# Wo's last weight sums, the first batch's inverse roots and the end's stores and routing in a fused post-LN layer

## The chip, the core and the metric

The kernel runs on one core of one Trainium2 chip, in one launch. The metric is device time in microseconds (us), as the median of three runs. The engines named below are PE (TensorE, matrix products), PEld (its weight loads), DVE (VectorE), ACT (ScalarE), POOL (GpSimd) and SP (SyncE, which issues most DMAs). All of them work through their own instructions in order; semaphores hold an instruction until its inputs are there and its output tile is free.

## The reference

Two batches of 512 tokens with 512 features pass through one layer, all in float32:

```python
q, k, v = (x @ W + b for Wq, Wk, Wv)          # 32 query heads, 8 key/value groups, 128 wide; rope on q and k
probs = softmax(causal(q k^T / sqrt(128)))
x1 = layernorm(x + (probs v) @ Wo + bo)
y  = x1 @ W_base^T + b_base
alpha = softmax(log(prior + eps) + x1 @ router_W^T + router_b)   # over 4 active experts
y += 2 * sum_e alpha_e * (x1 @ A_e^T) @ B_e^T                    # rank 8 each
out = layernorm(x1 + y)
```

A layernorm needs, per token, the mean, the variance and the inverse root of variance plus 1e-5.

## The kernel before

**Stages.** After a setup (about the first 60 us of the profile) comes a long loop over slots `T`. A slot scores 32 query rows of four heads against the keys (L546), and in the same slot come the row maxima (L554, DVE), exponentials (L561, ACT), normalisation (L569) and transposes (L577, L579) of slots just before, the weighing of values (L602), projections of later heads, and the output projection of earlier ones. Sixteen slots are one unit (one key group of one batch); there are 16 units, so 256 slots, `T_END = 256`. Four slots make one part, 128 tokens of four heads; a part's probabilities go out to DRAM and come back transposed (L587, L595, on SP). The order within a slot is written out by hand in `slot(T)`, and single steps are put at the end of a slot with `put(T, f)`; the schedule is taken as written. So every engine's order is the program's order.

**Products with seven instead of eight block multiplications.** Projections and the output projection use Strassen's scheme on 2 x 2 blocks, which needs sums of weight blocks and of data blocks first. For Wo these are `wo_sums`: four subtractions of 128x512 elements per set (L627), on DVE, into a tile `wt` of three blocks (`t1`, `t2`, `t4`; one buffer) and one in place (`b12`). A set is one key group's part of Wo. Sets 0 to 5 serve two units each; sets 6 to 9 serve one each. `wo_products` (L434) uses set `n` from slot `wo_from(first unit) = 16 u + 21`: its third product reads `t2` two slots on, the fourth reads `t1`, the fifth `b12`, the sixth `t4`. The sums of the data side, `ctx_sums` (L421 to L424), are on POOL, in the last slot before each new pair of heads. `rope_step` (L368, L371, L375 on DVE; L376 on POOL) and `w_sums` (L421 to L424 on POOL) run in the same slots. The last two units' output projection is plain (`wo_mm`, L674), so only sets 0 to 7 have sums, and only sets 6 and 7 of them serve a single unit (12 and 13).

**The second half of the layer.** The four token tiles of the first batch are finished while the second batch's last units are still in attention: `Ffn.stats` (L693, L694), `Norm.root` (an ACT square root at L697 and a DVE reciprocal at L698), `centre` (L701), `transpose` (L275, L276), `base` (L745), `logits`/`alphas` (L762 to L776), `low_rank`, `finish`, `add` (L796). They are put at slots counted from `A = 245`. Statistics of tiles 0 and 1 are at `A - 7` and `A - 6`, of 2 and 3 at `A`; one root for all four at `A + 1`. ACT holds the function tables of either the exponential or the square root, and an `ACT_TABLE_LOAD` stands before each change between them.

**The end.** After the loop the rest is written out line by line: `fz` is the first batch's last tile, `fa[0]`, `fa[1]`, `fb`, `fc` are the four tiles of the second batch in the order in which they end. `fc` is routed apart from its base product (`route`, L755: eight matmuls of 16 or 20 columns), and its base product is taken in two halves (L804) so that its statistics start early. Before the change the roots of `fz`, `fa[0]` and `fa[1]` stand together after `fa[1].add()`, followed by three stores (POOL applies the norm at L701, SP issues the DMA), and only then come `fb.logits()` and `fb.alphas()`.

Of the kernel before, what the change touches and what calls it, by code (L numbers as in the profile page):

```python
# [9 lines left out]
F32 = mybir.dt.float32  # L10
I32 = mybir.dt.int32
AF = mybir.ActivationFunctionType
ALU = mybir.AluOpType
AX = mybir.AxisListType

P = 128
# [7 lines left out]
LN_EPS = 1e-5  # L24
# [5 lines left out]
def postln_layer_kernel(  # L30
# [33 lines left out]
    nc = tc.nc  # L64
    B, S, HID = x.shape
    NT = B * S // P
    TPB = S // P
    KC = HID // P
    E_TOT, RK, _ = lora_A.shape
    O = W_base.shape[0]  # L70
    OC = O // P
    EA = active.shape[0]
    EAR = EA * RK
# [19 lines left out]
    def set_of(u):  # L93
        return u // B if u < MIXED else MIXED // B + u - MIXED

    def set_units(n):
        return [u for u in range(NU) if set_of(u) == n]
# [23 lines left out]
    OH, ARH = O // 2, EAR // 2  # L121
    WX_COLS = OH + ARH + EA
    arT = const.tile([P, KC, EAR + EA], F32, name="arT")
# [35 lines left out]
    def load_wo(n):  # L159
        wo_g = wow.tile([P, R, HID], F32, tag="wo_g", name=f"wo_{n}")  # L160
        nc.sync.dma_start(out=wo_g, in_=Wo[ts(sets[n], R * D), :].rearrange("(r p) n -> p r n", p=P))
        wos[n] = wo_g
# [455 lines left out]
    def wo_block(n, c_half, n_half):  # L618
        return wos[n][:, CH * c_half : CH * (c_half + 1), ts(n_half, NHALF)]

    def wo_sums(n, step):

        if step == 0:
            wt[n] = wow.tile([P, 3, CH, NHALF], F32, tag="wt", name=f"wt_{n}", bufs=1)
        t1, t2, t4 = (wt[n][:, m] for m in range(3))
        b11, b12, b21, b22 = (wo_block(n, c_half, n_half) for c_half in range(2) for n_half in range(2))
        nc.vector.tensor_tensor(  # L627
            *((t1, b12, b11), (t2, b22, t1), (b12, b22, b12), (t4, b21, t2))[step], ALU.subtract)

    def ctx_block(k, head, c_half):  # L630
# [52 lines left out]
    class Norm:  # L683
# [10 lines left out]
            nc.vector.bn_aggr(self.mv[:, i, :], st)  # L694

        def root(self, lo, hi):
            nc.scalar.activation(self.rstd[:, lo:hi], self.mv[:, lo:hi, 1], AF.Sqrt, bias=eps_sb)  # L697
            nc.vector.reciprocal(self.rstd[:, lo:hi], self.rstd[:, lo:hi])  # L698

        def apply(self, i, dst, src=None, engine=nc.vector):  # L700
            engine.tensor_scalar(  # L701
                dst, dst if src is None else src, self.mv[:, i, 0:1], self.rstd[:, i : i + 1], ALU.subtract, ALU.mult)
# [8 lines left out]
    class Ffn:  # L711
# [28 lines left out]
        def base(self, c):  # L740
            if c == 0:
                self.new_banks()
            for n in range(2):
                w = OH + (ARH, WX_COLS - OH)[n]
                nc.tensor.matmul(  # L745
                    self.py[n][:, :w], lhsT=self.xT[:, c, :], rhs=wbT[:, c, n, :w], start=(c == 0), stop=(c == KC - 1),
                    skip_group_check=True)

        def route(self, pool, tag):

            zl = pool.tile([P, 2, WX_COLS - OH], F32, tag=tag, name="zl")
            for n in range(2):
                w = (ARH, WX_COLS - OH)[n]
                for c in range(KC):
                    nc.tensor.matmul(  # L755
                        zl[:, n, :w], lhsT=self.xT[:, c, :], rhs=wbT[:, c, n, OH : OH + w],
                        start=(c == 0), stop=(c == KC - 1))
            self.z = [zl[:, n, :] for n in range(2)]

        def logits(self):  # L760
            self.lg = self.own([P, EA], "lg")
# [81 lines left out]
    def put(slot, f):  # L843
        extra.setdefault(slot, []).append(f)
# [59 lines left out]
    def wo_from(u):  # L904
        return UNIT * u + LAG_WO

    for n in range(2, NSETS):
        put(wo_from(set_units(n - 2)[-1] + 1) + 1, lambda n=n: load_wo(n))
    for n in range(NSETS - 2):
        for k in range(4):  # L910
            put(wo_from(set_units(n)[0]) + (0, 1, 1, 3)[k], lambda n=n, k=k: wo_sums(n, k))


    weigh_at = {}
# [139 lines left out]
    wbT = ffn_pool.tile([P, KC, 2, WX_COLS], F32, name="wbT")  # L1054
# [9 lines left out]
    def tiles(ts_, banks, name):  # L1064
        n = len(ts_)
        norms = Norm(ffn_pool, n, f"a{name}"), Norm(ffn_pool, n, f"f{name}")
        return [Ffn(t, bank, *norms, i) for i, (t, bank) in enumerate(zip(ts_, banks))]

    f0 = tiles(range(TPB), ((QX, QY), (QX, QY), (SC, SC), (QX, QY)), "0")
    fa = tiles([TPB + i for i in order[:2]], ((SC, SC), (WX, WY)), "1a")  # L1070
# [3 lines left out]
    A = LAST + LAG_WO  # L1074

    def transposed_base(c):
        transpose_token_tile(wbT[:, :, c // 2, ts(c % 2, P)], wb_sb[:, c, :], ps_k, "k", nc.scalar.copy)

    for c in range(OC):
        put(T_PROJ + (0, 1, 4, 5)[c], lambda c=c: nc.sync.dma_start(out=wb_sb[:, c, :], in_=W_base[ts(c, P), :]))  # L1080
        put(T_PROJ + (4, 5, 8, 9)[c], lambda c=c: transposed_base(c))
    put(A + 1, lambda: f0[0].norm1.root(0, TPB))
    for k, f in enumerate(f0):
        put(A + (-7, -6, 0, 0)[k], f.stats)
        put(A + 1 + k // 2, f.centre)
        put(A + 3 + k // 2, lambda f=f, k=k: f.transpose(*(QX, QY)[k % 2]))
    for f, at in zip(f0, (A + 5, A + 11, A + 13)):
# [11 lines left out]
    fz = f0[3]  # L1099
# [37 lines left out]
    fz.finish()  # L1137
    fc.transpose(*CTX)
    fz.add()
    base(fa[1])  # L1140
    fa[0].low_rank()
    fc.route(*CTX)
# [3 lines left out]
    fa[1].alphas()  # L1146
    fa[0].finish()
    fa[0].add()
    for c in range(KC):
        fb.base(c)  # L1150
        if c == 2:
            fa[1].low_rank()
    fc.low_rank()
    fa[1].finish()
    fa[1].add()
    fz.norm2.root(3, TPB)
    fa[0].norm2.root(0, 2)
    for f in (fz, *fa):
        f.store()
    fb.logits()  # L1160
    fb.alphas()
    for c in range(KC):
        fc.half(0, c)
    fc.half_end(0)
    fc.half_stats(0)
    fb.low_rank()
    for c in range(KC):
        fc.half(1, c)
# [59 lines left out]
```

## Time and profile before

| what | value |
|---|---|
| median of 3 runs | 831.65 us (830.76 to 831.83) |
| the profiled execution's own time | 829.5 us |
| its span, first to last recorded work | 827.4 us |
| PE, PEld busy | 99%, 72% |
| DVE, ACT, POOL busy | 73%, 46%, 38% |
| granted TensorE clock, mean | 0.998 |

The profile is of one execution. "Busy" is the time in which an engine has an instruction running; for PE the ends of matmuls are modelled, so the distance between starts is the better measure. Rows of the timeline give start, duration, engine, line and operation, output <- input, shape, count, and in brackets the idle time of the engine just before and what ended it. A float32 matmul is recorded as two rows, so "x4" of L434 is two matmuls.

### The profile page before, as it was taken

Reading aid. Unit: us, or ns where it says so; the run is one execution under the profiler, and the core shown is the slowest. Engines: PE = TensorE matmul, PEld = TensorE weight load, DVE = VectorE, ACT = ScalarE, POOL = GpSimd, SP = SyncE. Lnnn points to the kernel's source line nnn. Section 1 sums busy time; section 2 is a strip of 40 time slices with the busy share of each in tenths; the row PEclk is TensorE's granted clock in tenths of the full one; section 3 lists DMA queues with packets and bytes.
Section 4 is the critical chain, followed back from the end, with each engine's and each line's share of the span. In section 5 each row is a group of like instructions: output and inputs, shape, how many; then the busy total and the mean of one; then the engine's idle time right before and its main releaser. Section 6 shows DMA issues by size and latency. Waiting matters only on the chain.

```text
span 827.4 us, 11161 instructions
## 1 busy us (share of the span) xinstructions
PE 816.1 (99%) x3389; PEld 597.5 (72%) x3389; DVE 602.3 (73%) x1964; ACT 378.8 (46%) x1058; POOL 313.7 (38%) x342
## 2 busy tenths in 40 slices
PE   9999999999999999999999999999999999999996
PEld 5567777777777778787778778777778776645574
DVE  5368877677879886787768786787768789854545
ACT  1236454444545454444445354444445454663133
POOL 6464344421534345322533245442534433300032
PEclk9999999999999999999999999999999999999999
DMA  9015627444464547264554536374544546574211
GB/s 295 31 55 150 201 75 203 108 127 153 128 170 136 178 96 227 70 175 121 153 142 123 169 97 207 89 218 130 153 128 135 171 95 202 164 248 119 64 38 64
DMA packets 84413, 115.98 MB, mean 140 GB/s; under 512 B 6525, under 2 KB 64237, under 8 KB 82306
## 3 DMA queue, kind: packets, MB, share of 16 engines
q1 hardware_dynamic: 83682, 114.98, 48.2%
q8 instruction: 27, 0.44, 0.2%
q0 software_dynamic: 448, 0.14, 0.2%
q14 instruction: 32, 0.26, 0.1%
q10 hardware_dynamic: 224, 0.16, 0.1%
HBM read 71.21 MB, written 44.04 MB: 139 GB/s over the span
## 4 chain that ended last, share of the span: by engine, by line
PE 93%; DVE 4%; ACT 2%; issue 1%; POOL 1%; DVEq 0%; POOLq 0%
PE pc L602 16%; PE sc L546 14%; PE qx L434 11%; PE wx L434 11%; PE qy L434 9%; PE wy L434 8%; PE pp L355 5%; PE kx L434 4%; PE vx L512 4%; PE py L745 3%; PE po L674 3%; PE pv L338 3%; PE tp L275 1%; PE py L790 1%; DVE sc L554 0%
## 5 line engine op out<-in xcount | busy, mean ns | idle before, releaser
L554 DVE CUSTOM_DVE_ANT_0 sc<-sc,maskw 128x288 f32<-128x288 f32 (+15 forms) x256 | 114.2, 446 | 141.9 <-PE sc L546 140.3
L561 ACT ACTIVATE p<-sc,nmax 128x288 f32<-128x288 f32 (+15 forms) x256 | 124.1, 485 | 203.1 <-DVE nmax L554 180.9
L602 PE MATMUL pc<-pT,v 128*128 128x512 f32 x320 | 165.5, 599 | 0.0
L546 PE MATMUL sc<-kT,qT 128*128 128x160 f32 (+15 forms) x512 | 162.2, 399 | 1.7 <-ACT p L561 1.7
L376 POOL TENSOR_TENSOR qT<-q,t 128x512 f32<-128x512 f32 x56 | 76.9, 1372 | 179.9 <-DVE q L375 179.9
L569 ACT ACTIVATE p<-p,den 128x288 f32<-128x288 f32 (+15 forms) x256 | 133.2, 521 | 0.1
L546 PEld LDWEIGHTS sc<-kT,qT 128*128 128x128 f32 x512 | 95.9, 190 | 25.5 <-issue 8.6
L609 ACT ACTIVATE ctxT<-pc,bqkT 128x512 f32<-128x512 f32 x64 | 44.0, 687 | 116.4 <-PE pc L602 116.4
L421 POOL TENSOR_TENSOR cs<-ctxT 128x256 f32<-128x256 f32 x28 | 22.2, 794 | 157.8 <-PE wy L434 93.7
L577 DVE STREAM_TRANSPOSE zt<-p 128x128 f32<-128x128 f32 (+2 forms) x192 | 81.7, 425 | 0.0
L602 PEld LDWEIGHTS pc<-pT,v 128*128 128x128 f32 x320 | 57.0, 190 | 18.9 <-issue 5.7
L470 ACT COPY q<-qx 128x256 f32<-128x256 f32 x112 | 41.3, 369 | 36.6 <-PE qx L434 36.6
L434 PE MATMUL qx<-xs,wq 128*128 128x256 f32 x224 | 58.0, 381 | 0.0
L434 PE MATMUL wx<-wo,ctxT 128*128 128x256 f32 x224 | 57.6, 380 | 0.0
L434 PEld LDWEIGHTS qx<-xs,wq 128*128 128x128 f32 x224 | 41.4, 190 | 22.3 <-issue 18.4
L579 DVE STREAM_TRANSPOSE zt<-p 128x32 f32<-128x32 f32 (+3 forms) x256 | 57.5, 225 | 0.0
L561 ACT ACTIVATION_READ_ACCUMULATOR p<-sc,nmax 128x1 f32 x256 | 49.8, 195 | 0.0
L434 PEld LDWEIGHTS wx<-wo,ctxT 128*128 128x128 f32 x224 | 42.4, 190 | 7.8 <-issue 1.3
L660 DVE TENSOR_TENSOR x_sb<-wx,x_sb 128x256 f32<-128x256 f32 x112 | 47.0, 420 | 0.0
L368 DVE SCALAR_TENSOR_TENSOR t<-q,bqkT,rope_sb 64x512 f32<-64x512 f32 x56 | 45.0, 804 | 1.5
L701 POOL TENSOR_SCALAR y<-y,mv_f,rstd_f 128x512 f32<-128x512 f32 x4 | 8.5, 2129 | 94.2 <-DVE rstd_f L698 94.2
L371 DVE SCALAR_TENSOR_TENSOR t<-q,bqkT,rope_sb 64x512 f32<-64x512 f32 x56 | 42.2, 754 | 1.3
(215 smaller groups left out, 1505.7 us busy)
## 6 DMA issues: line engine op xcount, KB each, us to landing
db<-zt SPq DMA_DIRECT2D x64, 256.0 KB, 4.1
pT<-db SPq DMA_DIRECT2D x16, 1024.0 KB, 4.8
db<-zt SPq DMA_DIRECT2D x64, 192.0 KB, 3.1
pT<-db SPq DMA_DIRECT2D x16, 768.0 KB, 4.3
wq<-in_L_attn_Wq_dram SPq DMA_DIRECT2D x20, 512.0 KB, 5.3
wo<-in_L_attn_Wo_dram SPq DMA_DIRECT2D x10, 1024.0 KB, 7.6
db<-zt SPq DMA_DIRECT2D x64, 128.0 KB, 2.4
pT<-db SPq DMA_DIRECT2D x16, 512.0 KB, 4.0
```

The lines of the kernel that those rows point to most:

```text
L368: nc.vector.scalar_tensor_tensor(t2[lo, :], q[hi, :], b_ap[hi, :], rope_sb[hi, 1, :], ALU.add, ALU.mult)
L376: nc.gpsimd.tensor_tensor(dst, t1[:, :].rearrange("p (n s) -> p n s", s=BLK), t2[:, :].rearrange("p (n s) -> p n s", s=BLK), ALU.add)
L434: nc.tensor.matmul(ps, lhsT=wt[:, c, :], rhs=xt[:, c, :], start=start and c == 0, stop=c == CH - 1, skip_group_check=True)
L546: nc.tensor.matmul(sc[s][:, :w], lhsT=qT[u][:, i * QB + n].rearrange("p r s -> p (r s)"), rhs=kT[u][:].rearrange("p n s -> p (n s)")[:, :w ...
L554: nc.vector.tensor_tensor_reduce(sc[s][:, :w], sc[s][:, :w], maskw[:, S - w :], -SCALE, -MASKED, ALU.add, ALU.min, nmax[s])
L561: nc.scalar.activation(ptile[s][:, :w], sc[s][:, :w], AF.Exp, bias=nmax[s], scale=-1.0, accum_out=rden[s])
L569: nc.scalar.activation(ptile[s][:, :w], ptile[s][:, :w], AF.Copy, scale=rden[s])
L577: nc.vector.transpose(z[:, :, last - i : last, n, :].rearrange("p q j s -> p j q s"), ptile[s][:, : i * P])
L579: nc.vector.transpose(z[:, : n + 1, last, n, :], ptile[s][:, i * P : w])
L602: nc.tensor.matmul(psc[p], lhsT=v_sb[g // VG, b][:, j, ts(g % VG, D)], rhs=pT[p][:, :, ts(j, P)], start=(j == 0), stop=(j == i))
L609: nc.scalar.activation(ctxT[p], psc[p], AF.Identity, bias=bqkT[:, col : col + 1])
L660: nc.vector.tensor_tensor(into, pw[k, bank], into, ALU.add)
```

## The change

- `wo_sums` takes an engine. For the sets that serve one unit (6 and 7) all four subtractions go to POOL, at the end of slot `wo_from - 1`, behind that slot's `ctx_sums`; before they were on DVE at `wo_from` + 0, 1, 1 and 3.
- The first batch's four inverse roots are no longer a square root and a reciprocal. `newton` does four small DVE instructions (variance plus eps, its half negated, an integer shift, an integer subtraction that gives the first guess) and three Newton steps of four small POOL instructions each. It is called for tiles 0 and 1 at `A - 5` and for 2 and 3 at `A`, right behind their statistics.
- In the end, each root stands alone: `fz`'s root and store come right behind `fz.add()`; `fa[0]`'s square root behind `fa[0].add()`, its reciprocal and store behind `fc.low_rank()`; `fa[1]`'s square root behind `fa[1].add()`, its reciprocal and store behind the first half's statistics of `fc`. `fb.logits()` and `fb.alphas()` move ahead of `fa[1].finish()` and `fa[1].add()`.
- `route` is four matmuls of 36 columns from `arT` in place of eight from `wbT`.

```diff
-    def wo_sums(n, step):
+    def wo_sums(n, step, engine=nc.vector):
...
-        nc.vector.tensor_tensor(
+        engine.tensor_tensor(
             *((t1, b12, b11), (t2, b22, t1), (b12, b22, b12), (t4, b21, t2))[step], ALU.subtract)
...
+        def newton(self, lo, hi):
+            shape = [P, hi - lo]
+            v, w, t = (self.pool.tile(shape, F32, tag=f"newton_{n}", name=n, bufs=2) for n in "vwt")
+            y = self.rstd[:, lo:hi]
+            nc.vector.tensor_scalar(v, self.mv[:, lo:hi, 1], LN_EPS, None, ALU.add)
+            nc.vector.tensor_scalar(w, v, -0.5, None, ALU.mult)
+            bits = self.pool.tile(shape, I32, tag="newton_i", name="i", bufs=2)
+            nc.vector.tensor_single_scalar(bits, v[:].bitcast(I32), 1, op=ALU.logical_shift_right)
+            nc.vector.tensor_scalar(y.bitcast(I32), bits, -1.0, float(0x5F3759DF), ALU.mult, ALU.add)
+            for _ in range(3):
+                nc.gpsimd.tensor_tensor(t, y, y, ALU.mult)
+                nc.gpsimd.tensor_tensor(t, t, w, ALU.mult)
+                nc.gpsimd.tensor_scalar(t, t, 1.5, None, ALU.add)
+                nc.gpsimd.tensor_tensor(y, y, t, ALU.mult)
...
-            zl = pool.tile([P, 2, WX_COLS - OH], F32, tag=tag, name="zl")
-            for n in range(2):
-                w = (ARH, WX_COLS - OH)[n]
-                for c in range(KC):
-                    nc.tensor.matmul(
-                        zl[:, n, :w], lhsT=self.xT[:, c, :], rhs=wbT[:, c, n, OH : OH + w],
-                        start=(c == 0), stop=(c == KC - 1))
+            zl = pool.tile([P, EAR + EA], F32, tag=tag, name="zl")
+            for c in range(KC):
+                nc.tensor.matmul(zl, lhsT=self.xT[:, c, :], rhs=arT[:, c, :], start=(c == 0), stop=(c == KC - 1))
...
     for n in range(NSETS - 2):
+        single = len(set_units(n)) == 1
         for k in range(4):
-            put(wo_from(set_units(n)[0]) + (0, 1, 1, 3)[k], lambda n=n, k=k: wo_sums(n, k))
+            put(wo_from(set_units(n)[0]) + (-1 if single else (0, 1, 1, 3)[k]),
+                lambda n=n, k=k, engine=nc.gpsimd if single else nc.vector: wo_sums(n, k, engine))
...
-    put(A + 1, lambda: f0[0].norm1.root(0, TPB))
+    put(A - 5, lambda: f0[0].norm1.newton(0, 2))
     for k, f in enumerate(f0):
         put(A + (-7, -6, 0, 0)[k], f.stats)
+        if k == TPB - 1:
+            put(A, lambda: f0[0].norm1.newton(2, TPB))
...
     fz.add()
+    fz.norm2.root(3, TPB)
+    fz.store()
     base(fa[1])
...
     fa[0].add()
+    fa[0].norm2.sqrt(0, 1)
     for c in range(KC):
         fb.base(c)
         if c == 2:
             fa[1].low_rank()
     fc.low_rank()
+    fa[0].norm2.invert(0, 1)
+    fa[0].store()
+    fb.logits()
+    fb.alphas()
     fa[1].finish()
     fa[1].add()
-    fz.norm2.root(3, TPB)
-    fa[0].norm2.root(0, 2)
-    for f in (fz, *fa):
-        f.store()
-    fb.logits()
-    fb.alphas()
+    fa[1].norm2.sqrt(1, 2)
     for c in range(KC):
         fc.half(0, c)
     fc.half_end(0)
     fc.half_stats(0)
+    fa[1].norm2.invert(1, 2)
+    fa[1].store()
     fb.low_rank()
```

## The prediction

> **What bounds the kernel.** I read the page first, then busy time by stretches, then the timeline and the chain where PE is not full.
>
> ```profile
> PE 816.1 (99%) x3389; PEld 597.5 (72%) x3389; DVE 602.3 (73%) x1964; ACT 378.8 (46%) x1058; POOL 313.7 (38%) x342
> ...
> PE 93%; DVE 4%; ACT 2%; issue 1%; POOL 1%; DVEq 0%; POOLq 0%
> ```
>
> PE sets the end: what does not remove a PE instruction or a PE wait is worth nothing. The stretches (columns: length, then PE, PEld, DVE, ACT, POOL busy) show where PE waits:
>
> ```profile
> 640.00:660.00 20.00, 20.00 (x98) 16.05 (x97) 16.17 (x52) 8.24 (x26) 9.98 (x10) 1.00 0.62 184
> 692.00:696.00 4.00, 4.00 (x16) 2.59 (x15) 3.97 (x10) 0.76 (x3) 3.37 (x3) 1.00 0.57 188
> 696.00:700.00 4.00, 3.30 (x14) 2.18 (x12) 3.94 (x12) 1.93 (x6) 0.67 (x1) 1.00 0.97 349
> 735.00:745.00 10.00, 8.85 (x38) 5.03 (x37) 6.59 (x25) 7.47 (x18) 0.00 (x0) 1.00 0.73 221
> 815.00:827.40 12.40, 5.93 (x24) 3.54 (x22) 5.20 (x22) 5.11 (x9) 6.18 (x3) 0.89 0.28 106
> ```
>
> Set 6's sums (643.8 to 653.9) lie where PE is full; set 7's (692.2 to 701.9) where DVE is full and PE starts to wait; the root lies ahead of the gap after 735; the last row is the end.
>
> **Part 1: Wo's sums.** Rows from the timeline around set 7:
>
> ```profile
> 691.54 1.18 POOL L424 TENSOR_TENSOR ctxT<-ctxT,ctxT 128x256 f32<-128x256 f32 x1
> 692.68 1.72 POOL L376 TENSOR_TENSOR qT<-q,t 128x512 f32<-128x512 f32 x1
> 694.87 0.68 DVE L627 TENSOR_TENSOR wt<-wo,wt 128x512 f32<-128x512 f32 x1
> 695.02 1.65 POOL L376 TENSOR_TENSOR kT<-kT,t 128x512 f32<-128x512 f32 x1 [0.63 <-DVE kT L375]
> 695.47 1.75 DVE L627 TENSOR_TENSOR wo<-wo 128x512 f32<-128x512 f32 x1
> 697.92 1.13 PE L434 MATMUL wy<-wt,cs 128*128 128x256 f32 x4 [0.70 <-DVE x_sb L660]
> ```
>
> Removed from DVE for set 7: 1.11 + 0.68 + 1.75 + 0.69 = 4.2 us. PE's loss there I get from distances between starts where nothing waits: 0.86 for a pair of weighings or for four rows of 256 columns, 0.43 to 0.65 for scores 256 to 384 wide. From the weighing at 694.69 to the product at 706.95 stand five weighing pairs (4.30), four products (3.44) and five scores (2.70), 10.44 us in place of 12.26: 1.8 lost. From there to 726 the same sums give 1.4 more (0.33 at 714.7, 0.29 at 720.7, 0.35 at 722.4, the rest about 0.1 each). So 3.2 us are lost, mostly with DVE as the last wait.
>
> Added on POOL: four 128x512 subtractions. The same shape in L376 takes 1.26 to 1.27 us undisturbed (645.69, 656.64), so 5.2 with gaps. For set 6: without the DVE sums beside it, `ctx_sums` from 642.17 takes 4 x 0.78, L376 1.27, `t1` and `t2` 2 x 1.3, so `t2` is there at 649.2. PE wants it at 649.73: nothing gained or lost. Behind the sums POOL has `w_sums` for a product nine slots on and an L376 that starts at 656.64 after 5.38 us idle; both can wait 5 us. The load of the set's Wo is 30 slots old.
>
> For set 7 `t2` is late. [...]
>
> After that DVE carries 4.2 us less, and what it must do per slot (1.7 to 2.2 us, distances of L554 starts without L627) is about PE's own need (1.3 to 2.4). I keep 0.8 of loss to 726: the ACT wait at 720.7 stays, and Newton's first four DVE instructions (below) come in slot 240. So 1.6 + 0.8 against 3.2: **gain 0.8**, ends -0.8 (one more lock on the way to `t2`, and DVE stalls of its own) and +2.0 (no lock, no later loss).
>
> **Part 2: Newton.**
>
> ```profile
> 732.38 1.28 ACT L697 ACT_TABLE_LOAD   x1
> 735.10 1.28 ACT L561 ACT_TABLE_LOAD   x1
> 736.39 0.66 ACT L561 ACTIVATE p<-sc,nmax 128x480 f32<-128x480 f32 x1
> 737.20 0.41 PE L546 MATMUL sc<-kT,qT 128*128 128x32 f32 x2 [1.15 <-ACT p L561]
> ```
>
> The score at 737.20 needs the bank that the exponentials at 736.39 read. PE's last matmul before it starts at 734.17 and takes 4 x 0.43 = 1.72, so PE was free at 735.89: 1.3 lost. Without both loads and the root (2 x 1.28 + 0.3), and with no 4.92 us of DVE waiting for that root, these exponentials end at about 734.1 and the wait is gone.
>
> Added: twice four DVE instructions, nearest rows 0.16 (L772, 128x1) to 0.23 (L773, 128x4), so 0.8 a time; twice twelve dependent POOL instructions. POOL's L421 to L424 fall from 1.27 at 512 columns to 0.72 at 256, so about 0.17 at none; copies of 64 columns take 0.23 (L1055); with a gap of 0.08 between dependent ones that is about 0.27 each, 3.3 a time. POOL has nothing after 714.6. Tiles 0 and 1 are ready some twenty us before their `centre`. For tiles 2 and 3 DVE's part ends about 728.8 and POOL's about 732.1; DVE reaches their `centre` only behind L680, which waits for a product that ends about 733.3, so about 734.1. Newton's cover is that product: 2 us. **Gain 1.2** (0.1 off for the longer DVE queue), ends 0.6 and 1.3. After 745 PE is full to 815 and its DRAM round trips land 5 us or more ahead of use, so it passes through.
>
> **Part 3: the end.**
>
> ```profile
> 805.53 1.86 PE L755 MATMUL zl<-wbT,x1T 128*128 128x16 f32 x16
> ...
> 815.38 1.28 ACT L771 ACT_TABLE_LOAD   x1
> ...
> 817.87 0.28 PE L785 MATMUL tz<-ident,zs 128*32 128x128 f32 x1 [1.26 <-DVE zs L776]
> ```
>
> Routing: 16 rows in 1.70 us become 8. At 0.106 each, 0.85; by the score of 32 columns (two rows in 0.24), 0.96. I take 0.85, as 16 and 20 columns already run at the pace of the weight loads. Everything behind (fa[0]'s finish, fb's base, all later logits) comes 0.85 earlier.
>
> The wait of 1.26: `fb`'s exponential stood behind both roots and their table load. In the new order, all times 0.85 earlier: fz's table load, root and the load back take 802.4 to 805.3 on ACT, whose next work is at 807.0; hidden. The load for fa[0]'s root follows the exponential of fa[1] at 808.8; the root waits for statistics at 811.2; the load back ends at 812.75, 0.3 after `fb`'s logits are there. Then `zs` at 813.9, while PE comes to the transpose only at 815.75: 1.8 us of cover for a whole 1.28 load. fa[1]'s root at 815.6 has its table since 814.5, and the last two roots need no load. DVE waits 0.6 for fz's root (nothing due until 805.7) and not for the others. The moved stores bring two POOL runs of 2.1 us to about 804 and 812, when POOL is idle, and their DMAs to SP, where only other stores are queued. PE then reaches fb's finish at 816.85 in place of 818.95. **Gain 2.1**, ends 1.0 (POOL's stores lock out DVE once or twice) and 2.3.
>
> **Sum.** 0.8 + 1.2 + 2.1 = 4.1 us: the span goes from 827.4 to 823.3, the profiled execution from 829.5 to 825.4. The median of the runs lies 2.15 above the profiled one; I carry that over: 831.65 - 4.1 = **827.6**.
>
> **Rivals.**
> [...]
> 2. *Table loads take the wait's place at the end.* There are two loads more than before there. If fb's exponential is late by 1.8 or more, only the routing and a little else stay: part 3 about 0.3, in all 2.3: 829.4. Against: each load's place above has cover.
> 3. *Slower: Newton on POOL.* DVE's `centre` of tiles 2 and 3, and the row maxima behind it, wait for twelve dependent POOL instructions. Cover is 5.2 us from 728.9 to 734.1, and about 3 more until PE needs the bank that the next exponentials free. To lose 4.1 and 1.7 more takes 14 us, 1.17 each; at 1.4 each it would be 834. Against: no POOL row of few columns is over 0.24, except DMA issue. For it: none of these operations on so small a tile is in the trace.
>
> **How the numbers follow.** Chances: forecast 0.62, rival 1 0.18, rival 2 0.10, rival 3 0.10. What can be told from no change is 0.2%, 1.7 us, so faster is below 830.0. Rival 1 lies on that line (half each), rival 2 is mostly below it: faster 0.62 + 0.09 + 0.07 = 0.78, same 0.12, slower 0.10. The range: the best ends sum to 2.0 + 1.3 + 2.3 = 5.6, which is 826.0, and 0.2 for the median's own spread; upward it takes in rivals 1 and 2 with their spread: 825.8 to 830.6.
>
> **What would show it.** Right: the product on `t2` of set 7 waits for POOL 1 to 2 us near 696, and no DVE waits of 0.5 follow to 713; no table load between 730 and 740 and the 128x32 score starts without a wait; eight rows of L775 in 0.85; the transpose before fb's finish waits for nothing. Wrong: POOL rows of Newton over 0.45 each, PE waits for POOL at 649, DVE waits beyond 1 us at several places from 697 to 726, or an ACT wait ahead of fb's `zs`.

## The result

| | before | changed |
|---|---|---|
| median of 6 runs each | 831.76 us (830.76 to 833.51) | 826.43 us (825.83 to 827.88) |
| profiled execution | 829.5 us | 826.17 us |
| its span | 827.4 us | 824.2 us |

The ratio is 0.9936, with a 95% interval of 0.9923 to 0.9949: 5.3 us less. The forecast was 827.6 in a range of 825.8 to 830.6. Its time was nearly right, but the sum behind it was not: the two traces differ by 3.3 us, not by 4.1, and the medians by 5.3.

The page of the changed kernel, its first rows and its chain:

```profile
PE 814.9 (99%) x3381; PEld 596.9 (72%) x3381; DVE 598.2 (73%) x1964; ACT 379.0 (46%) x1058; POOL 327.8 (40%) x374
...
PE 94%; DVE 2%; POOL 2%; DMA 1%; ACT 0%; issue 0%; SPq 0%; DVEq 0%; POOLq 0%
```

DVE's share of the chain falls from 4% to 2% and ACT's from 2% to nothing; POOL has one point more and DMA is new. The same stretches as before the change (length, then PE, PEld, DVE, ACT, POOL busy, clock, DMA share, GB/s; the last begins at 812, as the end came forward):

```profile
640.00:660.00 20.00, 20.00 (x97) 16.03 (x96) 13.39 (x48) 8.45 (x27) 13.92 (x14) 1.00 0.62 184
692.00:696.00 4.00, 4.00 (x16) 2.52 (x14) 3.59 (x11) 0.51 (x2) 3.95 (x3) 1.00 0.52 171
696.00:700.00 4.00, 2.69 (x13) 2.34 (x13) 2.86 (x10) 2.30 (x8) 3.97 (x3) 1.00 0.91 336
735.00:745.00 10.00, 10.00 (x42) 5.80 (x41) 5.18 (x23) 5.40 (x16) 0.00 (x0) 1.00 0.70 251
812.00:824.20 12.20, 6.92 (x29) 4.47 (x27) 6.33 (x22) 3.53 (x8) 3.25 (x2) 0.91 0.23 86
```

Set 6 still lies where PE is full. At set 7 POOL, not DVE, is now the full engine, and PE is busy for 2.69 of 4 us instead of 3.30: worse. From 735 PE is full instead of 8.85 of 10. In the last 12 us PE has 6.92 us of work instead of 5.93, so it is less often held up there.

**Set 7**, timeline of the changed kernel:

```profile
693.01 1.26 POOL L376 TENSOR_TENSOR qT<-q,t 128x512 f32<-128x512 f32 x1
693.34 1.48 DVE L375 SCALAR_TENSOR_TENSOR kT<-kT,bqkT,rope_sb 128x512 f32<-128x512 f32 x1
694.24 1.72 POOL L627 TENSOR_TENSOR wt<-wo 128x512 f32<-128x512 f32 x1
696.03 1.26 POOL L627 TENSOR_TENSOR wt<-wo,wt 128x512 f32<-128x512 f32 x1
697.35 1.13 PE L434 MATMUL wx<-wt,cs 128*128 128x256 f32 x4 [1.31 <-POOL wt L627]
```

DVE's L375 starts under POOL's L376 and takes 1.48, where the same instruction on `q` takes 0.71 (at 689.00). Then `t1` starts under L375 and takes 1.72 instead of the 1.27 of `t4` (at 698.94). This slowing side by side is what the prediction and rival F below call a lock. `t2` ends at 697.29, and PE's product has waited 1.31 us for it.

**Newton**, tiles 2 and 3:

```profile
728.91 0.19 POOL L717 TENSOR_TENSOR t<-rstd_a 128x2 f32<-128x2 f32 x1 [7.13 <-DVE rstd_a L715]
...
732.38 0.20 POOL L720 TENSOR_TENSOR rstd_a<-rstd_a,t 128x2 f32<-128x2 f32 x1
733.87 0.69 DVE L680 TENSOR_TENSOR x_sb<-po,x_sb 128x512 f32<-128x512 f32 x1 [1.74 <-PE po L674]
734.48 0.99 DVE L723 TENSOR_SCALAR x_sb<-x_sb,mv_a,rstd_a 128x512 f32<-128x512 f32 x2
736.25 0.30 PE L546 MATMUL sc<-kT,qT 128*128 128x32 f32 x2
```

Twelve POOL instructions end at 732.58. DVE's `centre` (L723) shows no wait of its own: it stands behind L680, which waits for PE. The score of 32 columns shows no wait either; before it had one of 1.15.

**The end:**

```profile
804.48 0.98 PE L775 MATMUL zl<-arT,x1T 128*128 128x36 f32 x8
...
810.41 1.28 ACT L789 ACT_TABLE_LOAD   x1
811.71 0.30 ACT L789 ACTIVATE al<-lg,nmx 128x4 f32<-128x4 f32 x1
...
814.59 0.28 PE L803 MATMUL tz<-ident,zs 128*32 128x128 f32 x1
```

Eight rows instead of sixteen, a table load that ends at 811.69 just ahead of `fb`'s exponential, and a transpose of `zs` that waits for nothing.

Where the 3.3 us come from, by distances within each trace (so that an offset of 0.3 from earlier stages drops out):

| stretch on PE | before | changed | gained |
|---|---|---|---|
| 641, a product of set 6, to the score of 480 columns | 88.49 | 88.53 | 0.0 |
| that score to the score of 32 columns | 7.71 | 6.40 | 1.3 |
| first base product of `fa[1]` to the last store's issue, on ACT | 22.53 | 20.32 | 2.2 |

### The profile page after: what moved, and what is told of

Same layout as the page of the kernel before. It is cut to its first block, busy times and chain, and to the rows that moved or that the text cites. A ratio compares the mean times of both kernels' runs of the same rounds, so it can differ in the third digit from the quotient of the medians.

```text
span 824.2 us, 11178 instructions
## 1 busy us (share of the span) xinstructions
PE 814.9 (99%) x3381; PEld 596.9 (72%) x3381; DVE 598.2 (73%) x1964; ACT 379.0 (46%) x1058; POOL 327.8 (40%) x374
## 4 chain that ended last, share of the span: by engine, by line
PE 94%; DVE 2%; POOL 2%; DMA 1%; ACT 0%; issue 0%; SPq 0%; DVEq 0%; POOLq 0%
PE pc L602 16%; PE sc L546 14%; PE qx L434 11%; PE wx L434 11%; PE qy L434 9%; PE wy L434 8%; PE pp L355 5%; PE kx L434 4%; PE vx L512 4%; PE py L767 3%; PE po L674 3%; PE pv L338 3%; PE tp L275 1%; PE py L808 1%; DMA pT<-db 1%; DMA db<-zt 0%
## 5 line engine op out<-in xcount | busy, mean ns | idle before, releaser
L376 POOL TENSOR_TENSOR qT<-q,t 128x512 f32<-128x512 f32 x56 | 76.5, 1366 | 171.4 <-DVE q L375 171.4
L368 DVE SCALAR_TENSOR_TENSOR t<-q,bqkT,rope_sb 64x512 f32<-64x512 f32 x56 | 45.9, 820 | 1.5
L371 DVE SCALAR_TENSOR_TENSOR t<-q,bqkT,rope_sb 64x512 f32<-64x512 f32 x56 | 43.4, 775 | 1.3
L565 DVE RECIPROCAL den<-den 128x1 f32<-128x1 f32 x256 | 39.3, 153 | 1.5 <-ACT p L561 1.2
```

Of the source, the lines that this page charges most:

```text
L368: nc.vector.scalar_tensor_tensor(t2[lo, :], q[hi, :], b_ap[hi, :], rope_sb[hi, 1, :], ALU.add, ALU.mult)
L376: nc.gpsimd.tensor_tensor(dst, t1[:, :].rearrange("p (n s) -> p n s", s=BLK), t2[:, :].rearrange("p (n s) -> p n s", s=BLK), ALU.add)
```

## The experiments

Two things were open. Is part 1 really worth nothing, and why? And why did the medians move by 2 us more than the traces? Each kernel below was timed beside runs of the kernel before on the same chip.

**The parts one at a time**, and the kernel before with no edit (`before_again`).

> The kernel before once more, unchanged, for its own spread and a second trace. The profiled pair differs by 3.2 us of span (827.4 and 824.2), the medians by 5.3 (831.76 and 826.43). Theory A: the profiled execution of before was a quick one by about 2 us; a second trace has a span near 829.5 and shows where the 2 us come and go. Rival B: the trace of before is typical (span 827 to 828 again) and the 2 us lie outside the span. Time: ratio 1.000 within 0.2%.

```diff
 # only_sums: part 1 alone
-            put(wo_from(set_units(n)[0]) + (0, 1, 1, 3)[k], lambda n=n, k=k: wo_sums(n, k))
+            put(wo_from(set_units(n)[0]) + (-1 if single else (0, 1, 1, 3)[k]),
+                lambda n=n, k=k, engine=nc.gpsimd if single else nc.vector: wo_sums(n, k, engine))
```

> Only Wo's sums of sets 6 and 7 go to POOL. Theory A, read from the profiled pair (shared start point to the score 480 wide in the slot before Newton's tiles: 729.49 against 729.85, with 0.33 of offset before the change begins): PE's wait of 1.3 for POOL at 697 takes the place of the DVE waits, gain 0.0, 831.7 (830.9 to 832.5). Rival B, the recorded step: gain 0.8 (830.9) up to 2.0, and the median's missing 2 us lie here.

```diff
 # only_newton: part 2 alone
-    put(A + 1, lambda: f0[0].norm1.root(0, TPB))
+    put(A - 5, lambda: f0[0].norm1.newton(0, 2))
...
+        if k == TPB - 1:
+            put(A, lambda: f0[0].norm1.newton(2, TPB))
```

> Only Newton's iteration for the first batch's four roots. Both theories: the 1.3 us wait ahead of the 128x32 score goes, 1.2 to 1.3 gained, 830.5. A rival: the chance gain of this execution hides a loss, and the time is not under 831.3.

```diff
 # only_end: part 3 alone (routing, and the roots one by one)
     fz.add()
+    fz.norm2.root(3, TPB)
+    fz.store()
...
-    fz.norm2.root(3, TPB)
-    fa[0].norm2.root(0, 2)
-    for f in (fz, *fa):
-        f.store()
```

> Only the end: roots and stores one by one, fb's logits ahead of fa[1]'s add, routing in four matmuls. Theory A (trace of the pair, from the base product at 801.73 against 800.67 to the last store's issue at 824.26 against 820.99): 2.2 gained, 829.5. Rival B: the end gives more than the trace shows (stores that no longer crowd before the last one), 3.5 or more, 828.2.

| kernel | median, us | ratio to before, 95% interval |
|---|---|---|
| before_again | 831.18 | 1.0004, 0.9993 to 1.0015 |
| only_sums | 831.46 | 1.0004, 0.9993 to 1.0016 |
| only_newton | 830.03 | 0.9988, 0.9974 to 1.0003 |
| only_end | 827.49 | 0.9960, 0.9949 to 0.9971 |

Part 1 alone moves nothing. Part 2 gives 1.1; its interval just takes in no change, but its stretch in the trace gives 1.3 (from 7.71 to 6.39). Part 3 gives 3.7, in the range of its rival B, though its stretch in the trace gives 2.2. The surplus sits there. The 42 runs of the kernel before were not spread evenly either: 17 lie from 829.2 to 830.0, 25 from 831.0 to 833.9, and none between. Both `before_again` (span 828.9, near theory A's 829.5) and `only_newton` happened to be profiled in such a longer execution. The stretches of `before_again` (the column before the last two is the granted clock):

```profile
804.62:808.03 3.41, 3.41 (x25) 2.90 (x23) 0.61 (x4) 0.39 (x2) 0.00 (x0) 1.00 0.00 0
808.03:811.45 3.42, 3.42 (x8) 2.51 (x8) 2.75 (x13) 1.97 (x4) 0.00 (x0) 0.50 0.02 5
```

For 3.41 us TensorE has half its clock, and PE starts 8 rows there where the trace of `only_sums`, at full clock, has 16 in a stretch of the same length at the same place:

```profile
807.94:811.36 3.42, 3.42 (x16) 2.54 (x15) 2.60 (x13) 2.09 (x6) 0.00 (x0) 1.00 0.02 5
```

From the routing product (805.53 in the trace of before, 805.31 in that of `before_again`) to SP's last store it takes 18.58 us before and 20.21 in `before_again`: 1.63 lost (`only_newton`: 20.26, 1.68 lost). The two stores, of before and of `before_again`:

```profile
824.11 0.33 SPq L831 DMA_DIRECT2D out_dram<-y  x1
...
825.52 0.33 SPq L831 DMA_DIRECT2D out_dram<-y  x1
```

The clock changed at fixed distances. In the five traces with such a step, the full-clock and half-clock stretches recorded inside the execution are 1, 4, 5 and 235 times 3.413 us long (3413, 13653, 17067, 802132 ns); in the traces of before and changed, full clock lasts 819.2 and 815.8 us up to the half clock at their end, 240 and 239 times 3.413. So the steps of each of these executions lie on a grid of windows of 3.413 us. PE is recorded as busy for all of the window before the half-clock one (3.41 of 3.41 us in `before_again`). What fills that window is small products:

```profile
805.20 0.27 PE L785 MATMUL tz<-ident,zs 128*32 128x128 f32 x1
805.31 1.86 PE L755 MATMUL zl<-wbT,x1T 128*128 128x16 f32 x16
807.10 1.19 PE L790 MATMUL py<-bmT,zT 33*128 33x256 f32 x4
```

A transpose into 32 columns, sixteen rows of 16 or 20 columns, and rows that use 33 of 128 partitions: 3.0 us together, of which 2.83 lie in that window. That gave a theory to test (C below).

**Which half of part 3 brings the surplus?** `only_route` has only the routing in four matmuls, `only_roots` only the new order, and `after_old_route` is the changed kernel with the routing of before.

```diff
 # only_route, from the kernel before; after_old_route does the reverse to the changed kernel
-            zl = pool.tile([P, 2, WX_COLS - OH], F32, tag=tag, name="zl")
...
-                        zl[:, n, :w], lhsT=self.xT[:, c, :], rhs=wbT[:, c, n, OH : OH + w],
+            zl = pool.tile([P, EAR + EA], F32, tag=tag, name="zl")
+            for c in range(KC):
+                nc.tensor.matmul(zl, lhsT=self.xT[:, c, :], rhs=arT[:, c, :], start=(c == 0), stop=(c == KC - 1))
 # only_roots: the diff of only_end, with the eight matmuls of before
```

> The kernel before with only the routing of the last finish in eight products in place of sixteen. Theory C: in about 6 of 10 executions of the kernel before, TensorE runs one window of 3.413 us at half clock near 808, because the window ahead of it (804.6 to 808.0) is nearly filled by products of few columns or few rows: the transpose, the sixteen routing products and the bias product, 805.2 to 808.2; this costs 1.65 us, and with 0.9 us less of that work no window is so filled. Then the times are no longer split in two: 829.5 - 0.85 = 828.65, with at most 1 execution in 5 over 829.8; median 2.5 under that of before. Rival D: the half-clock window comes from elsewhere (the waits for roots, or chance). Then the times stay split as before, 828.6 and 830.3, and the median is 0.85 under that of before.

> The kernel before with only the new order of roots and stores at the end, and the sixteen routing products kept. Theory C: the times stay split in two, 829.5 - 1.3 = 828.2 and 829.9, about 6 of 10 in the upper half; median 1.3 under that of before. Rival D: with the wait of 1.26 us gone nothing is left that slows the clock: one group at 828.2, median 3 under that of before.

> The changed kernel with the sixteen routing products of before put back. Theory C: 0.9 us more of products and the split back: 827.3 and 828.9, median near 828.9 (0.9967 of before). Rival D: 827.3 in one group (0.9948 of before).

And the suspected cause doubled, in `after_old_route`; with it the changed kernel again:

```diff
 # route_doubled: every routing product twice, the second over the first
-            for n in range(2):
+            for n in (0, 1, 0, 1):
                 w = (ARH, WX_COLS - OH)[n]
```

> The changed kernel with the sixteen routing products of before, each issued twice (the second time over the first result, so the output is the same). Sixteen rows more at 0.106 are 1.7 us: 827.2 + 1.7 = 828.9 if nothing else happens. Theory C (a 3.413-us window nearly filled by small products brings a window of half clock): the stretch of small products is now 4.7 us, longer than a window whatever their offset, so at least three executions in four have the half-clock window, at 830.5 and over, and the profile shows it right behind the window that the stretch fills. Rival D (the window comes by chance or from elsewhere): about one execution in three at 830.5, the others at 828.9.

> The changed kernel once more, for the comparison with the three others on the same chip. Theory C: 826.4, at most one execution in five 1.3 us or more above the fastest group. Rival D: about one in three.

The result record of each execution has its mean granted clock. One half-clock window takes 3.413 x 0.5 / 828 = 0.002 off it, so the executions can be split at 0.998. The split errs in single executions: every trace also ends at half clock, for 0.35 us of its span (`before_again`) to 4.37 us (`only_newton`), and that enters the mean too. So the profiled execution of `before_again` reads 0.998 and yet has the half-clock window. For the 87 runs of the kernel before, the split agrees with the gap in their times (up to 830.58, and from 830.97).

| kernel | rows of the routing | median | at 0.998 or more: runs, median | below: runs, median |
|---|---|---|---|---|
| before (all runs beside these) | 16 | 831.29 | 33, 829.68 | 54, 831.62 |
| only_sums | 16 | 831.46 | 4, 829.49 | 10, 831.63 |
| only_newton | 16 | 830.03 | 6, 828.91 | 8, 830.29 |
| only_roots | 16 | 828.57 | 6, 828.34 | 2, 830.19 |
| after_old_route | 16 | 827.19 | 4, 827.15 | 2, 828.67 |
| route_doubled | 32 | 830.71 | 3, 828.58 | 9, 832.12 |
| only_route | 8 | 829.19 | 9, 828.80 | 5, 830.94 |
| only_end | 8 | 827.49 | 12, 827.48 | 1, 829.90 |
| changed | 8 | 826.43 | 5, 826.41 | 1, 827.88 |
| after_again | 8 | 826.61 | 5, 826.58 | 1, 827.94 |

At like clock the steps are those of the traces: routing 0.9, order of the roots 1.3, Newton 0.8, sums 0.2 or nothing, all together 3.3. The rest of the median's 5.3 is the share of executions with a lower clock: 54 of 87 before, 2 of 12 changed.

What decides that share? With 32 rows it is 9 of 12, as theory C expected (three in four; by its mark of 830.5 us it is 8, and a ninth ran 830.44); with eight rows, over all kernels, 11 of 61 (those of the table, `newton_nine` with 3 of 12, and `after_dve_sums` and `after_early`, below, with none of 5 each); with sixteen, 54 of 87 for the kernel before. But the small sets do not settle it. The median of `only_route` is 2.1 under that of before, nearer to theory C (2.5) than to rival D (0.85), yet 5 of its 14 executions have the lower clock where C had at most 1 in 5; `only_roots` (2.75 under) and `after_old_route` (827.19) went rival D's way. The traces tell the two apart better. For each of the 14 profiles, I took the stretch from the transpose to the next base product and the most of it that falls into one 3.413-us window of that execution's own grid:

```
                  rows   in one window   half-clock window behind it
route_doubled     32     3.41            yes
only_newton       16     2.96            yes
only_roots        16     2.95            yes
after_old_route   16     2.94            yes
before_again      16     2.83            yes
only_sums         16     2.66            no
before            16     2.18            no
newton_nine        8     2.07            no
six others         8     1.08 to 1.73    no
```

The order has no exception, and in each of the five the half clock begins at the end of that very window. In `route_doubled` the window is filled from end to end:

```profile
805.89:809.30 3.41, 3.41 (x26) 3.02 (x26) 0.43 (x3) 0.39 (x2) 0.00 (x0) 0.99 0.22 82
809.31:812.72 3.41, 3.41 (x9) 2.55 (x9) 2.75 (x13) 1.67 (x3) 0.00 (x0) 0.51 0.00 0
```

`only_roots` and `after_old_route`, which keep the sixteen rows and lack the late wait, both show the half clock in the same place, and the wait of before (at 817.87) comes only after that place. So the window does not need rival D's late wait. With eight rows the stretch is only 2.08 long and cannot fill 2.83 of a window. The limit, somewhere from 2.66 to 2.83, is read off these same profiles; only the one of `route_doubled` was forecast.

How often the window comes is not explained. With a limit of 2.75 and an evenly spread offset of the grid, a stretch of 2.96 would fill a window in (3.41 - 2.96 + 2 x 0.2) / 3.41 of the executions, a quarter, and the 4.76 of `route_doubled` in (3.41 - (2 x 2.75 - 4.76)) / 3.41, or 0.78; both are estimates. The second fits 9 of 12. The first fits `only_roots` and `after_old_route` (4 of 14 together), but not the kernels with sixteen rows and the late wait (`before`, `only_sums` and `only_newton`: 72 of 115). So the order of the roots goes with the share in a way that theory C does not give, and that stays open. What slowed the 11 of 61 executions of eight-row kernels wasn't profiled and stays open too.

**Part 1 undone, and part 1 earlier.**

```diff
 # after_dve_sums, from the changed kernel
-            put(wo_from(set_units(n)[0]) + (-1 if single else (0, 1, 1, 3)[k]),
-                lambda n=n, k=k, engine=nc.gpsimd if single else nc.vector: wo_sums(n, k, engine))
+            put(wo_from(set_units(n)[0]) + (0, 1, 1, 3)[k], lambda n=n, k=k: wo_sums(n, k))
 # after_early, from the changed kernel: slots before wo_from
-            put(wo_from(set_units(n)[0]) + (-1 if single else (0, 1, 1, 3)[k]),
+            put(wo_from(set_units(n)[0]) + ((-2, -2, -1, -1) if single else (0, 1, 1, 3))[k],
```

> The changed kernel with its first part undone: all sums of Wo's blocks on VectorE, as before. Theory A: the first part is worth nothing, since the 1.3 us that PE waits for POOL at 697 are as much as the waits that it takes away: 826.4, within 0.4. Rival: the parts are not independent, and with the inverse roots off VectorE the sums on VectorE cost less than they did (825.6) or, with Newton's four instructions there, more (827.2).

> The changed kernel with the four sums on POOL issued one unit earlier for sets 6 and 7. Theory E: part 1 is worth nothing because PE waits 1.3 us at 697 for the last of POOL's differences; issued earlier they are ready in time, and the loss is gone: 826.4 - 1.3 = 825.1. Rival F: the loss only moves, since POOL locks VectorE out at another place and the waits up to 726 grow by as much: 826.4, within 0.4. A third outcome, slower: the earlier sums meet the evictions of the unit before and PE waits there as well, 827 or more.

"One unit earlier" means one slot here, and only for the first two: `t1` and `t2` are put one slot earlier, ahead of `ctx_sums` instead of behind them, and `b12` and `t4` stay where they were.

`after_dve_sums`: 826.42 (826.29 to 826.98), the changed kernel's time. Part 1 is worth nothing, with the other parts as without them.

`after_early`: 824.52 (824.28 to 824.88), ratio to before 0.9924, 0.9911 to 0.9938. It beats both kernels: its five runs all lie under the fastest of the changed kernel (825.83), and its median is 1.9 lower, though on another chip. Its timeline around set 7:

```profile
686.78 1.45 POOL L627 TENSOR_TENSOR wt<-wo 128x512 f32<-128x512 f32 x1 [3.81 <-PE wx L434]
688.30 1.60 POOL L627 TENSOR_TENSOR wt<-wo,wt 128x512 f32<-128x512 f32 x1
689.87 1.18 POOL L421 TENSOR_TENSOR cs<-ctxT 128x256 f32<-128x256 f32 x1
695.52 1.03 PE L434 MATMUL wx<-wt,cs 128*128 128x256 f32 x4
```

POOL was idle for 3.81 us there, and starts as soon as PE has read the old `wt`. Beside DVE's L371 and L368 the two subtractions take 1.45 and 1.60 us, together no less than in the changed kernel (1.72 and 1.26), but `t2` is ready at 689.9 and PE's product starts on time at 695.52. From the weighing (694.66) to the product on `wo` and `cs` (705.60) PE takes 10.94 us: 0.5 lost instead of 1.7. From 641 to the score of 480 columns it gains 1.4, as theory E had it (1.3); the remaining 0.5 of the median lies in the 0.35 by which this trace is early already at 641, and in the runs' spread.

**Newton's cover priced.**

```diff
 # newton_nine, from the changed kernel
-            for _ in range(3):
+            for _ in range(9):
                 nc.gpsimd.tensor_tensor(t, y, y, ALU.mult)
```

> The changed kernel with nine Newton steps a call on POOL in place of three (24 more dependent instructions a call at 0.27 us: 6.5 us more). The second call is ready at 728.9 + 9.8 = 738.7 and DVE's centring of tiles 2 and 3 moves from 734.5 to there. Theory G: of these 4.2 us of lateness about 3 are covered until PE needs the bank that the next exponentials free, as the prediction's third rival has it: 826.4 + 1.2 = 827.6. Rival H: DVE's queue is all that PE has to feed on there, so nearly all of it arrives at PE: 826.4 + 4 = 830.4. A third outcome: PE has more in store than thought, 826.4.

828.62, against 826.61 for the changed kernel on the same chip: 2.0 slower, between theory G (1.2) and rival H (4), nearer to G.

```profile
739.24 1.00 DVE L723 TENSOR_SCALAR x_sb<-x_sb,mv_a,rstd_a 128x512 f32<-128x512 f32 x2 [4.63 <-POOL rstd_a L720]
...
741.77 0.43 PE L546 MATMUL sc<-kT,qT 128*128 128x64 f32 x2 [1.65 <-ACT p L561]
```

Counted from the product at 641 (641.18 here, 641.32 in the changed kernel), DVE centres 4.9 us later than in the changed kernel, where it was at 734.48, and PE comes to the routing product 2.1 us later. So 2.8 us were covered, beyond the 1.9 between POOL's end (732.58) and L723.

## Why the prediction was right and wrong

**Part 1: no gain, 0.8 predicted.** What was to be seen near 696 came. Set 6's `t2` was ready at 649.3 with PE asking at 650.05 and not waiting. At set 7 POOL's L376, DVE's L375, `t1` and `t2` ended one after the other, at 694.27, 694.82, 695.96 and 697.29, and PE's product waited 1.31 for POOL. No run shows the 1.6 that the sum takes for this delay; by distances between starts, the changed kernel shows 697.29 - (695.01 + 0.86) = 1.4 in its place. Up to the product on `wo` and `cs`, 1.7 us are lost (12.15 - 10.44); before it was 1.8. So there the wait for POOL took the place of the waits for DVE.

The term that failed is "I keep 0.8 of loss to 726". It runs from that product to the score of 480 columns; before, then changed:

```profile
706.95 1.03 PE L434 MATMUL wy<-wo,cs 128*128 128x256 f32 x4
729.49 0.97 PE L546 MATMUL sc<-kT,qT 128*128 128x480 f32 x2
...
707.16 1.03 PE L434 MATMUL wy<-wo,cs 128*128 128x256 f32 x4
729.85 0.97 PE L546 MATMUL sc<-kT,qT 128*128 128x480 f32 x2
```

That is 22.54 us before and 22.69 changed: none of the 1.4 went away, and the loss is 1.7 + 1.5 against 3.2. The stretch takes 22.40 to 23.32 in the seven traces with set 7's sums on DVE and 22.35 to 22.89 in the seven with them on POOL (22.49 in `after_early`), so these losses do not depend on where the sums are. I had put them down mostly to a full DVE. What PE waits for stands at its weight loads, here of the changed kernel:

```profile
714.86 0.73 PEld L434 LDWEIGHTS wy<-wt,cs 128*128 128x128 f32 x4 [0.94 <-DVE x_sb L660]
717.18 0.73 PEld L434 LDWEIGHTS wx<-wo,ctxT 128*128 128x128 f32 x4 [0.68 <-DVE x_sb L660]
720.87 0.42 PEld L275 LDWEIGHTS tp<-ident,wb_sb 128*128 128x128 f32 x4 [0.69 <-ACT wbT L276]
722.57 0.30 PEld L546 LDWEIGHTS sc<-kT,qT 128*128 128x128 f32 x2 [0.59 <-ACT p L561]
725.12 0.30 PEld L602 LDWEIGHTS pc<-pT,v 128*128 128x128 f32 x2 [0.74 <-DMA pT<-db]
```

The kernel before has the same five waits, 0.99, 0.68, 0.69, 0.59 and 0.54 long. Two end on DVE, two on ACT and one on a DMA, and 4.2 us less for DVE up to 702 shortened none by more than 0.05. The prediction's sign of being right, no DVE waits of 0.5 up to 713, came true, but it stops short of where the term failed. For the last of the five, the chain of the changed kernel shows (start, length, what):

```profile
716.79 3.94 DMA db<-zt
720.77 0.03 issue
720.80 4.28 DMA pT<-db
725.08 0.04 issue
725.12 1.13 PE pc L602 x2
```

PE's weighing at 725.12 stands behind two DMA legs of 8.2 us in all, so a delay on DVE some ten us earlier could surface there; no run tests that.

**Part 2: right, 1.2 predicted and 1.3 in the trace** (1.1 in the medians of `only_newton`, not clear of noise). The POOL instructions took 0.19 to 0.24 and mostly started 0.27 to 0.30 apart (two took 0.38, beside DVE's L723), as estimated from the rows of 256 columns; POOL was done at 732.58 against 732.1, and DVE's centring began at 734.48 against 734.1. The third rival needed 1.17 us per instruction. (Its 834 for 1.4 us each is a slip: 12 x 1.4 less 8.2 of cover is 8.6 lost, and 827.6 + 8.6 is 836.) Its cover of "about 3 more" was measured at 2.8.

**Part 3: right, 2.1 predicted and 2.2 in the trace.** Apart, the routing gives 0.88 (from the routing product to the last store 17.70 instead of 18.58; predicted 0.85) and the order 1.3 (16.36 with both, in the trace of `only_end`; predicted 1.26). The loads fell where the steps had them, a little earlier, and the second rival's late exponential didn't come: 811.71.

**The median.** "The median of the runs lies 2.15 above the profiled one; I carry that over" is the other step that failed. The difference is not a constant of the measurement but a property of the kernel: of the kernel before, the profile shows an execution without the half-clock window, and most runs (54 of 87) had a lower clock. The changed kernel's median lies 0.26 above its profiled time. So the forecast was 0.8 too hopeful in one place, 1.9 too cautious in the other, and landed within 1.2. That these two errors partly cancel was luck; parts 2 and 3 were not.

## What to carry to other kernels

When work moves to another engine, ask first when its inputs are free and where that engine is idle, not only what it takes: the same four subtractions were worth nothing at one slot, and 1.4 us of PE time with the first two of them one slot earlier. A loss that lies behind a busy engine is not yet caused by it: look at which wait ends last in that stretch before crediting the relief. And where a median lies well above the profiled execution, split the runs by granted clock before carrying the difference over.

## What was not expected of the hardware

In mid-run, TensorE's clock fell to half (0.50) for one window of 3.413 us though PE has no idle time in the records of the window before. In 14 profiles this came in all 5 where 2.83 us or more of a window went to products of few columns or few partitions, and in none of the 9 with 2.66 or less. It cost 1.63 and 1.68 us where it could be measured against an undisturbed trace. How often it comes, and by what rule, no run here shows.
